# Another slot order, clamped-distance pairs by content, and score tiles partly filled by VectorE, in a fused attention and mixture-of-experts kernel

## The chip, the cores and the metric

The kernel runs on one core of a Trainium2 chip. The metric is the device time of one execution in microseconds, the median of several runs. The profile is of one further execution, with the time of each instruction on the five engines: PE (TensorE, the matrix engine; PEld is its loading of stationary operands), DVE (VectorE), ACT (ScalarE), POOL (GpSimd) and SP (SyncE, which here issues nearly all transfers).

## The reference

Sixteen sequences of 512 tokens with 256 features go through an adaptive LayerNorm, self-attention with 16 heads of 16, a second LayerNorm, and a mixture of eight experts of which each token uses two. All is float32. What matters here are the attention scores with relative positions:

```python
scores = jnp.einsum('bhqd,bhkd->bhqk', q, k)
dist_idx = pos_l - pos_r + M - 1            # M = 256, S = 512
pos_emb = dist_emb[dist_idx]
rel_q = jnp.einsum('bhld,lrd->bhlr', q, pos_emb)
rel_k = jnp.einsum('bhrd,lrd->bhlr', k, pos_emb)
scores = (scores + rel_q + rel_k) / jnp.sqrt(jnp.asarray(D, scores.dtype))
probs = jax.nn.softmax(scores, axis=-1)
```

The table dist_emb has 511 rows, and an index out of range takes the nearest row. All pairs whose query is 255 or more positions after the key thus use row 510. Call it e. For these pairs the three terms are q·k + q·e + k·e, which equals (q + e)·(k + e) − e·e.

## The kernel before, in words

**The prologue** (until about 490 us) normalizes the inputs, projects them to q, k and v, stores these in DRAM, rearranges q and k for the position terms (`stationary`), and works the first ten *pair blocks* off.

**Pair blocks** make the position terms rel_q + rel_k. A block (`Rel`, number n of 64) is 64 queries by 128 keys for the 128 pairs of batch and head of one half s of the batches; `at(n)` gives half, query block lb, key block rb and half lh of the query block. `q_set` (matmul L165, "pq" in the profile) makes rel_q for 16 queries in four PSUM banks, one for each group t of 32 rows of the array, and four ScalarE copies (L175) move them to an SBUF block `two[n % 2]` ("r"). `k_set` (L186, "pk") makes rel_k in four banks in the same way, and four VectorE additions (L195) add them to r. `store` (L203) writes 16 queries of r to rel_d in DRAM in 1 MB. Four of each make a block. A store has runs of 128 floats in DRAM.

**Units** are 128 queries of one sequence; there are 64, and each takes 16 *slots*. In groups g of four heads: `load_scores` (L582) reads position terms for 4 x 512 scores a query into a tile s, in one transfer. `content` makes q·k in four banks (L644, "qk"), and VectorE adds s to each, scales, and keeps the maximum of each row (L650); the negated maximum is the bias of `exps` (L660, ScalarE). `turn` transposes the four probability tiles on PE (L669, "pt") and ScalarE copies each out (L671). `context` multiplies them with v (L684, "pc") in a bank of its own.

The unit before goes through its second part in the same slots. `back`, `contextT` and `project` finish the attention (pcl, pct, ph). `project` copies ph on ScalarE (L738), and takes its statistics on VectorE (L741) and the inverse root on POOL (L101). `residual` scales on VectorE (L750) and makes three POOL operations (L751 to L753). `norm2` follows with statistics, an inverse root on POOL and xn (L765). `modulate`, `route`, `mask_t` and `bias` prepare the experts. `experts` multiplies for two experts at once into one bank (L827, "fpy"), and `expert_sums` adds the first half on VectorE (L838, "fy") and scales the second on ScalarE (L842, "ye"); POOL adds up ye. `mask_q` (L614, POOL) makes the two masked copies of q for the next unit.

**The order** is written by hand. `at(slot, order, fn, ...)` puts a call in a slot, and the calls of a slot are issued by their order number. The engines then take their instructions in that order. Slots repeat by fours, once for each head group. Modulo 4, PE's order was:

- slot 0: pt, then qk of the next group
- slot 1: pt, then pc of the last group
- slot 2: pt, pq, fpy (and exps of two head tiles on ScalarE, after the pq copies)
- slot 3: fy and ye, then pk, then pt (and two more exps)

Work that comes once per unit (ph in slot 7, fpt in 11, fpl in 13 and so on) lies between. Block n = u + 10 is made during unit u.

All PSUM tiles but pc's come from one pool of seven banks, `bank()`, taken in turn: a matmul group that takes a bank waits until the readers of the bank taken seven allocations earlier are done. A transfer on SP uses one of eight completion lanes in turn, and waits for the last on its lane.

## Time and profile before

| | |
|---|---|
| median of 3 runs | 2924.61 us (2921.96 to 2926.6) |
| profiled execution, its time / its span | 2935.72 / 2934.0 us |
| busy: PE, PEld | 2770.9 us (94%), 1803.2 us (61%) |
| busy: DVE, ACT, POOL | 1837.4 us (63%), 2068.8 us (71%), 630.1 us (21%) |
| granted TensorE clock, mean | 0.971 |
| SP's queue: moved, share of 16 engines | 790.03 MB, 85.2% |
| position terms: stores, loads | 256 of 1 MB each |

The busy share of a waiting matmul group needs care: its first matmuls can have begun while the others wait, and the record shows the group as busy. The shares are means over a prologue, a middle in which every unit carries a pair block, and a tail of ten units without one.

### The profile page before, as it was taken

Reading aid. Unit: us, or ns where it says so; the run is one execution under the profiler, and the core shown is the slowest. Engines: PE = TensorE matmul, PEld = TensorE weight load, DVE = VectorE, ACT = ScalarE, POOL = GpSimd, SP = SyncE. Lnnn points to the kernel's source line nnn. Section 1 sums busy time; section 2 is a strip of 40 time slices with the busy share of each in tenths; the row PEclk is TensorE's granted clock in tenths of the full one; section 3 lists DMA queues with packets and bytes.
Section 4 is the critical chain, followed back from the end, with each engine's and each line's share of the span. In section 5 each row is a group of like instructions: output and inputs, shape, how many; then the busy total and the mean of one; then the engine's idle time right before and its main releaser. Section 6 shows DMA issues by size and latency. Waiting matters only on the chain.

```text
span 2934.0 us, 76492 instructions
## 1 busy us (share of the span) xinstructions
PE 2770.9 (94%) x30186; PEld 1803.2 (61%) x30186; DVE 1837.4 (63%) x5140; ACT 2068.8 (71%) x3938; POOL 630.1 (21%) x863
## 2 busy tenths in 40 slices
PE   8779963999999999999999999999999999999997
PEld 5556642666666666666666666666666666665654
DVE  5446542666666666666666666666666666675553
ACT  2345432877777777777777777777777777777774
POOL 1000000022222222222222222222222222223333
PEclk9989876999999999999999999999999999999998
DMA  6879998688988998899888998889899898897561
GB/s 181 306 253 317 296 299 273 223 276 283 286 282 277 294 307 279 274 285 292 281 278 286 291 289 281 278 285 288 278 286 307 279 286 281 278 278 264 201 238 43
DMA packets 855350, 796.49 MB, mean 271 GB/s; under 512 B 25545, under 2 KB 649409, under 8 KB 854737
## 3 DMA queue, kind: packets, MB, share of 16 engines
q1 hardware_dynamic: 854032, 790.03, 85.2%
q8 instruction: 240, 3.93, 0.5%
q10 hardware_dynamic: 960, 1.57, 0.2%
q14 instruction: 118, 0.96, 0.1%
HBM read 462.20 MB, written 328.25 MB: 269 GB/s over the span
## 4 chain that ended last, share of the span: by engine, by line
PE 77%; DMA 2%; POOL 2%; DVE 1%; SPq 1%; ACT 1%; issue 1%; POOLq 0%; DVEq 0%; ACTq 0%
PE pt L669 18%; PE fpy L827 15%; PE qk L644 12%; PE pq L165 10%; PE pc L684 8%; PE pk L186 8%; PE ph L732 2%; DMA vu<-v_d 1%; PE fpl L788 1%; PE pcl L699 1%; PE fpb L818 1%; PE fpt L775 1%; POOL qm L614 1%; PE pct L716 0%; POOL rstd L101 0%
## 5 line engine op out<-in xcount | busy, mean ns | idle before, releaser
L671 ACT COPY pT<-pt 128x512 f32<-128x512 f32 x1024 | 595.3, 584 | 317.9 <-PE pt L669 295.3
L195 DVE TENSOR_TENSOR r<-pk,r 128x512 f32<-128x512 f32 x1024 | 635.0, 683 | 189.2 <-PE pk L186 164.3
L660 ACT ACTIVATE s<-s,mx 128x512 f32<-128x512 f32 x1024 | 689.7, 731 | 43.3 <-DVE mx L654 39.7
L650 DVE CUSTOM_DVE_ANT_0 s<-qk,s 128x512 f32<-128x512 f32 x1024 | 644.1, 685 | 85.8 <-PE qk L644 81.4
L669 PE MATMUL pt<-ident,s 128*128 128x128 f32 x4096 | 660.0, 284 | 10.8 <-ACT s L660 10.4
L175 ACT COPY r<-pq 128x512 f32<-128x512 f32 x1024 | 525.6, 603 | 153.9 <-PE pq L165 137.1
L669 PEld LDWEIGHTS pt<-ident,s 128*128 128x128 f32 x4096 | 450.0, 143 | 284.7 <-ACT s L660 73.8
L827 PE MATMUL fpy<-we_sb,fhT 128*128 128x512 f32 x1024 | 506.1, 617 | 0.0
L848 POOL TENSOR_TENSOR ye<-ye,ye 128x256 f32<-128x256 f32 x192 | 140.5, 732 | 1597.4 <-ACT ye L842 1105.8
L838 DVE SCALAR_TENSOR_TENSOR fy<-fpy,fmask,fy 128x256 f32<-128x256 f32 x256 | 123.5, 482 | 471.6 <-PE fpy L827 319.3
L644 PE MATMUL qk<-k,qm 32*128 32x512 f32 x2048 | 380.1, 650 | 28.0 <-POOL qm L614 28.0
L186 PEld LDWEIGHTS pk<-t_f,ke 32*128 32x128 f32 x8192 | 268.3, 190 | 189.5 <-ACT r L175 124.1
L165 PE MATMUL pq<-t_r,qe 32*128 32x256 f32 x4096 | 370.5, 409 | 4.2 <-DMA qe<-eq_d 2.8
L186 PE MATMUL pk<-t_f,ke 32*128 32x128 f32 x8192 | 319.8, 287 | 8.8 <-DVE r L195 3.6
L827 PEld LDWEIGHTS fpy<-we_sb,fhT 128*128 128x128 f32 x1024 | 175.0, 190 | 195.2 <-issue 159.8
L165 PEld LDWEIGHTS pq<-t_r,qe 32*128 32x128 f32 x4096 | 240.2, 186 | 82.4 <-issue 41.7
L684 PE MATMUL pc<-pT,vu 128*32 128x128 f32 x8192 | 279.1, 277 | 0.0
L684 PEld LDWEIGHTS pc<-pT,vu 128*32 128x32 f32 x8192 | 209.9, 110 | 44.1 <-issue 43.5
L644 PEld LDWEIGHTS qk<-k,qm 32*128 32x128 f32 x2048 | 133.4, 184 | 101.5 <-DVE r L195 47.6
L101 POOL TENSOR_TENSOR rstd<-rstd,mhalf 128x1 f32<-128x1 f32 (+1 forms) x144 | 87.9, 610 | 436.0 <-DVE rstd L100 428.1
L842 ACT ACTIVATE ye<-fpy,fmask 128x256 f32<-128x256 f32 x256 | 125.3, 490 | 51.3 <-DVE fy L838 51.3
L614 POOL TENSOR_SCALAR qm<-qs,par 128x256 f32<-128x256 f32 x128 | 117.7, 932 | 150.1 <-DMA k<-k_d 137.8
(110 smaller groups left out, 2061.7 us busy)
## 6 DMA issues: line engine op xcount, KB each, us to landing
rel_d<-r SPq DMA_DIRECT2D x256, 1024.0 KB, 8.5
s<-rel_d SPq DMA_DIRECT2D x256, 1024.0 KB, 7.8
vu<-v_d SPq DMA_DIRECT2D x64, 576.0 KB, 7.5
ke<-ek_d SPq DMA_DIRECT2D x128, 256.0 KB, 7.2
k<-k_d SPq DMA_DIRECT2D x128, 256.0 KB, 6.6
gt<-gates_d SPq DMA_DIRECT2D x64, 256.0 KB, 4.7
v_d<-v SPq DMA_DIRECT2D x16, 576.0 KB, 6.4
xt<-in_x SPq DMA_DIRECT2D x16, 512.0 KB, 5.9
```

Of the source, the lines that this page charges most:

```text
L165: nc.tensor.matmul(bs[t][:, a * 256 : (a + 1) * 256], e[32 * t : 32 * t + 32, (g % 2) * 2 + a, :], t_r[32 * t : 32 * t + 32, :, m0 : m0 + RK],
L175: nc.scalar.copy(dst[:, t], bs[t].rearrange("p (a c) -> p a c", a=2))
L186: nc.tensor.matmul(bs[t][:, a * 128 : (a + 1) * 128], e[32 * t : 32 * t + 32, a, :], t_f[32 * t : 32 * t + 32, :, m0 : m0 + LQ], start=Tru ...
L195: nc.vector.tensor_tensor(dst, bs[t].rearrange("p (r l) -> p l r", r=8), dst, ALU.add)
L614: nc.gpsimd.tensor_scalar(qm[:, pa], qs, par[:, pa : pa + 1], None, ALU.mult)
L644: nc.tensor.matmul(bs[t], t_["q"][rows, pa, cc, :], t_["k", cc][rows, :], start=True, stop=True)
L650: nc.vector.tensor_tensor_reduce(st[:, t, :], bs[t], st[:, t, :], 0.25, -3.0e38, ALU.add, ALU.max, mx[:, t : t + 1],)
L660: nc.scalar.activation(t_["s", g][:, t, :], t_["s", g][:, t, :], AF.Exp, bias=t_["m", g][:, t : t + 1])
L669: nc.tensor.transpose(pt[:, cols], t_["s", g][:, t, cols], ident)
L671: nc.scalar.copy(pT, pt)
L684: nc.tensor.matmul(pc[32 * t : 32 * t + 32, g, :], t_["v"][:, rb, h * VW : h * VW + 32], pTs[t][:, rb * P : (rb + 1) * P], start=(rb == 0) ...
L827: nc.tensor.matmul(py, t_["hT"][:, kc, :], we_sb[:, kc, pr * 2 * E : (pr + 1) * 2 * E], start=(kc == 0), stop=(kc == NE - 1),)
```

## The change

1. *Pairs at the clamped distance.* For query block 3 and key block 0 all distances are 257 or more. The four blocks with n % 32 in 24, 25 are left out (`todo`, 60 blocks). For query block 3, `content` uses two matmuls for each t: the plain one for the last 384 keys, and one with q + e (`qf`, made on POOL) and k + e (`shift_k`, in place, on POOL) for the first 128. The −e·e is put in the score tile by VectorE.
2. *rel_d's layout.* It is now [head, key block, query, 128 keys]. A store of 16 queries is one run of 8 KB a head, and the load of a head group is four transfers, one for each head, with runs of 512 B.
3. *Another order of the four slots*, and pq's four copies in two pairs. Modulo 4 it is now: slot 0: pt, pc, qk; slot 1: pt; slot 2: pt, fpy, the first exps, fy and ye, pq and its first two copies; slot 3: pt, pq's other two copies, pk, the other three exps.
4. *One buffer* instead of two for the first ye of a unit (`ye0`).

The core of it:

```diff
-    rel_d = [dram.tile([P, P, S], F32, tag=f"rel_{n}", name=f"rel_d{n}") for n in range(8)]
+    rel_d = [dram.tile([P, NL, P, RK], F32, tag=f"rel_{n}", name=f"rel_d{n}") for n in range(8)]
...
+            self.todo = [n for n in range(64) if n % 32 // 2 != 12]
...
+            self.banks = bs
+            self.q_copy(n, g, (0, 1))
+
+        def q_copy(self, n, g, ts):
...
-            for t in range(4):
-                nc.scalar.copy(dst[:, t], bs[t].rearrange("p (a c) -> p a c", a=2))
+            for t in ts:
+                nc.scalar.copy(dst[:, t], self.banks[t].rearrange("p (a c) -> p a c", a=2))
...
-                out=rel_d[s * 4 + lb][:, l0 : l0 + 16, rb * RK : (rb + 1) * RK],
+                out=rel_d[s * 4 + lb][:, rb, l0 : l0 + 16, :],
...
-        nc.sync.dma_start(
-            out=st, in_=rel_d[s * 4 + lb][h0 : h0 + 7 : 2].rearrange("h l r -> l h r")
-        )
+        rb0 = lb // 3
+        r0 = RK * rb0
+        for t in range(4):
+            nc.sync.dma_start(
+                out=st[:, t, r0:].rearrange("p (rb r) -> p rb r", r=RK),
+                in_=rel_d[s * 4 + lb][h0 + 2 * t, rb0:].rearrange("rb l r -> l rb r"),
+            )
+        if r0:
+            nc.vector.tensor_copy(
+                st[:, :, 0:r0], minus_ee.unsqueeze(2).to_broadcast([P, 4, r0])
+            )
...
+    def shift_k(u, cc):
+        kt = units[u]["k", cc]
+        nc.gpsimd.tensor_scalar(kt[:, 0:RK], kt[:, 0:RK], far, None, ALU.add)
...
+        if place(u)[1] == 3:
+            qf = u1.tile([P, 2, NE, P], F32, tag="qf", name=f"qf_{u}")
+            for pa in range(2):
+                nc.gpsimd.tensor_scalar(
+                    qf[:, pa], qs, far, par[:, pa : pa + 1], ALU.add, ALU.mult
+                )
...
+            r0 = RK if "qf" in t_ else 0
             nc.tensor.matmul(
-                bs[t], t_["q"][rows, pa, cc, :], t_["k", cc][rows, :], start=True, stop=True
-            )
+                bs[t][:, r0:], t_["q"][rows, pa, cc, :], t_["k", cc][rows, r0:],
+                start=True, stop=True,
+            )
+            if r0:
+                nc.tensor.matmul(
+                    bs[t][:, 0:r0], t_["qf"][rows, pa, cc, :], t_["k", cc][rows, 0:r0],
+                    start=True, stop=True,
+                )
...
-        ye = u2.tile([P, E], F32, tag=f"ye{pr > 0}", name=f"ye_{u}_{pr}")
+        ye = (u2 if pr else u1).tile([P, E], F32, tag=f"ye{pr > 0}", name=f"ye_{u}_{pr}")
...
             at(q0 - 4, 5, content, u, g)
-            at(q0 - 2, 7, exps, u, g, (0, 1))
-            at(q0 - 1, 7, exps, u, g, (2, 3))
+            at(q0 - 2, 6.3, exps, u, g, (0,))
+            at(q0 - 1, 5, exps, u, g, (1, 2, 3))
             for t in range(4):
                 at(q0 + t, 3, turn, u, g, t)
-            at(q0 + 5, 4, context, u, g)
+            at(q0 + 4, 4, context, u, g)
...
+        if u % 32 // 8 == 3:
+            at(z - 8, 0, shift_k, u, 0)
+            at(z - 2, 0, shift_k, u, 1)
...
-        at(z + 16, 7, bias, u)
+        at(z + 17, 6, bias, u)
         for pr in range(4):
             at(z + 18 + 4 * pr, 6, experts, u, pr)
-            at(z + 19 + 4 * pr, 1, expert_sums, u, pr)
+            at(z + 18 + 4 * pr, 6.6, expert_sums, u, pr)
...
-                at(z + 2 + 4 * g, 4, rel.q_set, n, g)
-                at(z + 15 + 4 * g, 2, rel.k_set, n, g)
+                at(z + 2 + 4 * g, 7, rel.q_set, n, g)
+                at(z + 3 + 4 * g, 3.5, rel.q_copy, n, g, (2, 3))
+                at(z + 15 + 4 * g, 4, rel.k_set, n, g)
```

The rest of the diff makes `far` (e on the 128 rows) and `minus_ee` in the prologue, where all four pq copies still follow `q_set` at once, and counts the blocks by `todo`.

More of the change, by code (lines that the diff above doesn't have):

```diff
@@ L94, in adaln_attention_moe_kernel @@
     t_r = const.tile([P, 2, 2 * S], F32, name="t_r")
+    far = const.tile([P, 1], F32, name="far")
+    minus_ee = const.tile([P, 4], F32, name="minus_ee")
     wo_sb = const.tile([P, NE, E], F32, name="wo_sb")
@@ L131, in __init__, with at @@
             self.ke = {}
+            self.todo = [n for n in range(64) if n % 32 // 2 != 12]
             self.two = [rblk.tile([P, LQ, RK], F32, name=f"r_{i}") for i in range(2)]
-        @staticmethod
-        def at(n):
-            s, m = n // 32, n % 32
+        def at(self, n):
+            s, m = self.todo[n] // 32, self.todo[n] % 32
             return s, m // 8, m % 8 // 2, m % 2
@@ L142, in wants @@
             w = []
-            if rb == 0:
+            if rb == lb // 3:
                 w += [("q", s, lb * 2 + lh, g) for g in range(2)]
@@ L383, in blocks @@
                 rel.q_set(n, g)
+                rel.q_copy(n, g, (2, 3))
                 for w in ahead:
@@ L514, in adaln_attention_moe_kernel @@
                     )
+            far_row = su.tile([P, D], F32, name="far_row")
+            last = dist_t[:, 510:511]
+            with nc.allow_non_contiguous_dma(reason="one column of the table"):
+                nc.sync.dma_start(
+                    out=far_row, in_=last.rearrange("d o -> (o d)").partition_broadcast(P)
+                )
+            for h in range(8):
+                nc.sync.dma_start(out=far[h * D : (h + 1) * D, :], in_=last)
+            nc.vector.tensor_tensor(far_row, far_row, far_row, ALU.mult)
+            nc.vector.tensor_reduce(
+                minus_ee, far_row.unsqueeze(1).to_broadcast([P, 4, D]), AX.X, ALU.add
+            )
+            nc.vector.tensor_scalar(minus_ee, minus_ee, -1.0, None, ALU.mult)
             m8 = su.tile([P, 8], F32, name="m8")
@@ L581, in load_scores @@
         st = sp.tile([P, 4, S], F32, tag="s", name=f"s_{u}_{g}")
-        nc.sync.dma_start(
-            out=st, in_=rel_d[s * 4 + lb][h0 : h0 + 7 : 2].rearrange("h l r -> l h r")
-        )
+        rb0 = lb // 3
+        r0 = RK * rb0
+        for t in range(4):
+            nc.sync.dma_start(
+                out=st[:, t, r0:].rearrange("p (rb r) -> p rb r", r=RK),
[5 more added lines that the diff above has]
+            )
         units[u]["s", g] = st
@@ L615, in mask_q @@
         units[u]["q"] = qm
+        if place(u)[1] == 3:
[4 more added lines that the diff above has]
+                )
+            units[u]["qf"] = qf
     def load_rest(u):
@@ L643, in content @@
             rows = slice(32 * t, 32 * t + 32)
+            r0 = RK if "qf" in t_ else 0
             nc.tensor.matmul(
-                bs[t], t_["q"][rows, pa, cc, :], t_["k", cc][rows, :], start=True, stop=True
-            )
+                bs[t][:, r0:], t_["q"][rows, pa, cc, :], t_["k", cc][rows, r0:],
+                start=True, stop=True,
+            )
+            if r0:
+                nc.tensor.matmul(
+                    bs[t][:, 0:r0], t_["qf"][rows, pa, cc, :], t_["k", cc][rows, 0:r0],
+                    start=True, stop=True,
+                )
         mx = u3.tile([P, 4], F32, tag="mx", name=f"mx_{u}_{g}")
@@ L899, in adaln_attention_moe_kernel @@
         n = u + LEAD
-        if n < NP:
+        if n < len(rel.todo):
             for g in range(4):
-                at(z + 2 + 4 * g, 4, rel.q_set, n, g)
-                at(z + 15 + 4 * g, 2, rel.k_set, n, g)
+                at(z + 2 + 4 * g, 7, rel.q_set, n, g)
+                at(z + 3 + 4 * g, 3.5, rel.q_copy, n, g, (2, 3))
+                at(z + 15 + 4 * g, 4, rel.k_set, n, g)
             for g in range(4):
                 at(z + 28 + 2 * g, 0, rel.store, n, g)
-        if n + 1 < NP:
+        if n + 1 < len(rel.todo):
             for w in rel.wants(n + 1):
```

## The prediction

> **What bounds the kernel now.** I read the page's engine rows first, then its chain of work that ended last, then one stretch in the middle and one near the end.

> ```profile
> span 2934.0 us, 76492 instructions
> PE 2770.9 (94%) x30186; PEld 1803.2 (61%) x30186; DVE 1837.4 (63%) x5140; ACT 2068.8 (71%) x3938; POOL 630.1 (21%) x863
> PE 77%; DMA 2%; POOL 2%; DVE 1%; SPq 1%; ACT 1%; issue 1%; POOLq 0%; DVEq 0%; ACTq 0%
> 1400.00:1600.00 200.00, 199.99 (x2337) 129.55 (x2341) 133.41 (x370) 157.28 (x302) 47.42 (x65) 1.00 0.90 281
> 2700.00:2800.00 100.00, 94.04 (x923) 60.42 (x923) 57.82 (x198) 76.95 (x148) 33.33 (x46) 0.98 0.65 230
> ```

> TensorE sets the time: 199.99 of 200 us busy in mid-kernel. But a group of matmuls that waits for one PSUM bank still counts as busy, so I took the timeline of one unit (repeats every 39.1 us) and measured from each group's start to the next one's. Around the LayerNorms it reads, PE first, then DVE, POOL and ACT:

> ```profile
> 1520.97 1.17 PE L186 MATMUL pk<-t_f,ke 32*128 32x128 f32 x32
> 1527.47 2.02 PE L165 MATMUL pq<-t_r,qe 32*128 32x256 f32 x16
> 1529.42 1.98 PE L827 MATMUL fpy<-we_sb,fhT 128*128 128x512 f32 x4
> 1531.33 1.17 PE L186 MATMUL pk<-t_f,ke 32*128 32x128 f32 x32
> ...
> 1522.16 2.49 DVE L195 TENSOR_TENSOR r<-pk,r 128x512 f32<-128x512 f32 x4 [0.60 <-PE pk L186]
> 1524.57 0.42 DVE L741 BATCH_NORM_STATS2 stats<-ph 128x6 f32<-128x256 f32 x1
> 1531.28 0.42 DVE L765 TENSOR_SCALAR xn<-x,mv,rstd 128x256 f32<-128x256 f32 x1 [1.18 <-POOL rstd L101]
> 1531.61 0.48 DVE L838 SCALAR_TENSOR_TENSOR fy<-fpy,fmask,fy 128x256 f32<-128x256 f32 x1
> ...
> 1526.56 0.74 POOL L751 TENSOR_TENSOR x<-x,gt 128x256 f32<-128x256 f32 x1 [0.53 <-DVE x L750]
> 1528.88 1.83 POOL L614 TENSOR_SCALAR qm<-qs,par 128x256 f32<-128x256 f32 x2
> 1530.68 0.57 POOL L101 TENSOR_TENSOR rstd<-rstd,mhalf 128x1 f32<-128x1 f32 x1
> ...
> 1529.11 2.06 ACT L175 COPY r<-pq 128x512 f32<-128x512 f32 x4 [0.89 <-PE pq L165]
> 1532.26 0.49 ACT L842 ACTIVATE ye<-fpy,fmask 128x256 f32<-128x256 f32 x1
> ```

> The same pq group takes 1.08 us start to start where nothing holds it; here 1.95. Over the four groups of the unit, qk and pq lose 2.4 us above 1.08 (qk 0.54 and 0.75; pq 0.08, 0.18 and 0.87). The cause is the ring of seven PSUM banks: the last bank of qk is the one that pk's third VectorE add (L195) empties, seven allocations earlier; pq's last bank is emptied by the third score reduction. So mid-kernel is about 36.7 us of matmuls plus 2.4 us of such waits. The second thing to see is a long chain: stats (24.57), POOL's gate products, POOL's qm, POOL's rstd (30.68), xn, fy (ends 32.09). It is 7.52 us, and today it delays nobody in mid-kernel. In the tail, with less PE work, it does:

> ```profile
> 2858.50 0.44 PE L775 MATMUL fpt<-ident,xn 128*128 128x128 f32 x2 [1.86 <-DVE xn L765]
> ```

> [...] in the trace ye never begins less than 0.035 us after fy's end, in 256 pairs. [...] So everything behind a waiting ye on ScalarE waits too. [...] the gaps of 1.86 us in the tail go with a granted clock of 0.98. I add nothing for that.

> **The change part by part.** T is a transpose group, F the expert matmul (fpy); t is microseconds from where pk could start.

> *Slot order.* PE ran T, qk, T, pc, T, pq, F, pk, T. It becomes T, pc, qk, T, T, F, pq, T, pk. Switch costs: T takes 0.49 before T or F and 0.58 before others; 0.1 per group less, 0.4 per unit. qk's last banks now come from pk's first two adds, with T (0.58) and pc (1.01) between: no wait. pq's banks come from score reductions with T, T, F (2.9 us) between: none. Those 2.4 us go. But pk's third and fourth banks are now the two that pq's first copies empty, with only one T between. From the rows: the first copy starts 1.16 us after pq does, the second 0.48 later (four take 2.06), and takes 0.60: free at 2.24, with semaphore 2.28. PE reaches pk at 1.08 + 0.58 = 1.66. Wait 0.62, in every group. The four a-rounds of pk issue in order, so the whole pk slips, and the adds begin at t = 1.57 instead of 1.19.

> *fy and ye move before pq's copies.* In an ordinary group this is hidden: fy starts 0.11 after F's successor, ends 0.59, ye runs 0.63 to about 1.1, the first copy is due at 1.16. In the LayerNorm group it isn't. ScalarE, in order, does two pq copies, T's copy, two pq copies, three exps (0.62 apart), then the copy of ph: it ends at t = 4.16, and the bn_stats on the same bank follows at 4.2. Plus 7.52: fy ends at 11.72. PE meanwhile: pk to 1.72, ph 1.11, T 0.58, pc 1.01, qk 1.08, T and T 0.98, F 1.91, pq 1.08, T 0.58: ready for pk at 10.05. ye starts 11.76, copies at 12.16 and 12.64, the second ends 13.24: pk's last bank opens at 13.28, a wait of 3.2. In the router group nine small VectorE instructions (1.38 us) stand between the reductions and fy: fy ends about 1.1 us after F, the wait is 1.0. Sum per unit: 0.62 + 0.62 + 3.2 + 1.0 = 5.5, for 2.4 + 0.4 gained: period 41.8, **+2.7 us**. About 49 periods have pair work: **+132**.

> *Four pair blocks left out.* Four periods with pair work become periods without. The last ten units of before run at 28.5 or 30.1, mean 29.3: 4 x (39.1 - 29.3) = **-39**. Their adds, copies, stores and stationary loads go with them.

> *Content with q+e and k+e.* 256 matmuls become 512 of 384 and 128 columns: the columns are the same, and pk shows that 128-column matmuls on four row groups cost no extra (32 in 1.10 us). Nothing added, at most 0.2 us x 64 = 13. On POOL, qf is two more instructions like qm (0.93 each) and the shift of k is half of one (0.5): 2.4 us ahead of rstd in the chain above, so fy and pk are later by that much in 16 units: **+38**. The second shift lies in a stretch where POOL idles. The VectorE fill (512 elements, like a 0.68 us row) comes 64 times, ahead of the score reductions; VectorE is 63% busy and pq has 0.4 us to spare: nothing, at most 40.

> *rel_d's layout and four loads for one.* A 1 MB store goes from 2048 packets of 512 B to 128 of 8 KB. In the trace's packet records 512 B take 28.7 ns, 2 KB 96, 8 KB 309 (medians and means near each other): over 16 engines 3.7 us becomes 2.5. A load goes from 512 packets of 2 KB (3.1 us) to 2048 of 512 B (3.7). Per unit that is -4.8 and +2.4: 35 us of DMA work become 32.5, in a longer period. In mid-kernel transfers are early, so nothing. In the prologue, from 220 to 490 us, the DMA share is 0.9 to 1.1 and 40 stores lie there, worth 48 us; I take **-35** (bounds 0 and -55). SP issues 12 more DMAs a unit at about 0.45 us: 5.4 us; the waits of its stores alone (565.9 us in 58) show 10 us of slack a unit. The small setup loads: 0 to 3.

> *Tail.* Without pq and pk, pc comes one slot earlier and needs T's copy, which is behind ye: reductions and negation end 2.8 us after qk, exp0, then fy and ye end at 4.0, T's copy at 4.5, while PE is there at 4.1: 0.4 to 0.5 a group. In the LayerNorm group ph's copy is behind three exps, so the 1.86 us gap grows by about 1. Some 32.2 us a unit for 29.3, 14 units: **+41**.

> *ye with one buffer.* Its last reader ends some 2.5 us into the four slots before the next writer: nothing; if not, up to 1 us a unit.

> **Sum.** 2934 - 35 + 132 - 39 + 38 + 41 = 3071 for the profiled execution. The execution profiled took 2935.7 against a median of 2924.6, so the median is 9 less than this sum: **3062**.

> **The rivals.** (1) *Faster: fy does not hold the copies.* Place: fy, ye, pq's copies. It decides if the 7.5 us chain finishes before F ends, at t = 8.4, that is, if it were 4.2 us shorter. Then each wait is 0.62: 4 x 0.62 - 2.4 - 0.4 = -0.3 a unit, -15; with -35, -39 and +10 in the tail, about 2846. For it: the chain costs nothing in mid-kernel now. Against: xn waits 1.18 us for POOL there, and fy is behind xn in the built order. (2) *DMA becomes the bound.* 33 DMAs a unit on eight completion lanes, each waiting for the one eight before it. At the 7.8 us to landing of today 33 x 7.8 / 8 = 32 us, plus 10 of waits: 42, just the new period. If 512 B reads land in 10 us it is 51 a unit, about 3500. Against: fewer bytes are queued ahead of each. (3) *Half of it*: the three exps and the copy of ph overlap better than I have it, or the shifts find POOL idle: about 2990.

> **How the numbers follow.** The forecast's mechanism 0.70, half of it 0.11, DMA 0.04, the faster one 0.12, balance near zero 0.03. Between runs this kernel varies by 0.16%, so 0.2% is what can be told from no change. Slower 0.85, same 0.03, faster 0.12. The forecast's own range is 3010 to 3125 (prologue 0 to -55, fill and content 0 to +50, tail 0 to +60). The half case takes it down to 2940, and I stop there, as what lies below and above is under 2 in 10; upper end 3130.

> **What would show it.** qk and pq groups at 1.08 us or a little more; pk groups at 1.7 us in two of four, about 2.1 after the router and 4.3 after the LayerNorm; PE's waits named ACT r or ACT ye at pk; DMA share down to about 0.8; the first pair of qk some 35 us earlier; period 41.8. Wrong would be: pk at 1.10 after the LayerNorm (then rival 1), s loads as the releaser of the score reductions (rival 2), a period below 39.1.

## The result, and the profile after

The changed kernel takes **3219.47 us** (median of 4 runs, 3218.88 to 3224.17) against 2925.61 us of the kernel before in the same session (4 runs, 2921.96 to 2928.58). The ratio is 1.1009, with a 95% interval of 1.099 to 1.1028: ten per cent slower. The forecast had the direction, and the place of the new waits, but its rise of 137 us is less than half of the 294 us measured.

The profiled execution spans 3217.2 us, 283.2 more than before. First the page of the changed kernel: the engine rows, the shares of engines in the chain of work that ended last, and SP's queue.

```profile
span 3217.2 us, 77690 instructions
PE 2927.8 (91%) x29930; PEld 1935.5 (60%) x29930; DVE 1823.6 (57%) x5143; ACT 2021.2 (63%) x3874; POOL 665.3 (21%) x927
q1 hardware_dynamic: 734112, 754.43, 73.0%
PE 12%; POOL 4%; DVE 3%; issue 2%; DMA 2%; ACT 1%; SPq 1%; POOLq 0%; DVEq 0%; ACTq 0%
```

ScalarE and VectorE do less than before in a longer span, and SP's queue falls from 85.2% to 73.0% of the engines' time. So no engine and no queue has become fuller. The chain explains only a quarter of the span by name (before, PE alone was 77% of it), so it doesn't say where the time went. The view by stretches (length, busy time of PE, PEld, DVE, ACT and POOL, granted TensorE clock, DMA share, GB/s) shows a stretch in the middle and one in the tail:

```profile
1000.00:1200.00 200.00, 192.50 (x2092) 125.03 (x2090) 122.16 (x336) 138.70 (x269) 43.56 (x60) 0.97 0.82 262
2900.00:3000.00 100.00, 82.19 (x821) 57.66 (x820) 49.08 (x166) 61.78 (x118) 32.54 (x47) 0.90 0.51 154
```

Before, PE was busy for 199.99 of 200 us in mid-kernel, with 2337 matmuls at a clock of 1.00. Now it begins 2092, has 7.5 us with nothing at all, and its clock is 0.97.

The unit shows why. This is the timeline of the group around the LayerNorms, the stretch that the forecast was made from (start, duration, engine, line, operation; in brackets the idle time before it and what ended it):

```profile
1100.27 1.78 PE L194 MATMUL pk<-t_f,ke 32*128 32x128 f32 x32
1106.69 1.88 PE L877 MATMUL fpy<-we_sb,fhT 128*128 128x512 f32 x4
1108.50 1.47 PE L169 MATMUL pq<-t_r,qe 32*128 32x256 f32 x16
1110.49 0.48 PE L194 MATMUL pk<-t_f,ke 32*128 32x128 f32 x2
1112.51 2.95 PE L194 MATMUL pk<-t_f,ke 32*128 32x128 f32 x30 [1.54 <-ACT ye L892]
1115.39 0.69 PE L825 MATMUL fpt<-ident,xn 128*128 128x128 f32 x2
...
1104.43 0.43 DVE L791 BATCH_NORM_STATS2 stats<-ph 128x6 f32<-128x256 f32 x1
1111.14 0.41 DVE L815 TENSOR_SCALAR xn<-x,mv,rstd 128x256 f32<-128x256 f32 x1 [1.17 <-POOL rstd L104]
1111.47 0.48 DVE L888 SCALAR_TENSOR_TENSOR fy<-fpy,fmask,fy 128x256 f32<-128x256 f32 x1
...
1111.98 0.47 ACT L892 ACTIVATE ye<-fpy,fmask 128x256 f32<-128x256 f32 x1 [1.99 <-DVE fy L888]
1112.35 1.06 ACT L183 COPY r<-pq 128x512 f32<-128x512 f32 x2
```

From bn_stats (1104.43) to the end of fy (1111.95) it is again 7.52 us, as before. But fpy, which fy reads, ended at 1108.5, so fy comes 2.9 us late, ye follows fy, the first two copies of pq follow ye, and pk stands between 1110.97 and 1112.51 with its first two matmuls issued. The single records of pk show which banks it waits for: its second bank is that of fpy and opens with the end of ye (1112.45, pk goes on at 1112.51), and its third and fourth are those of pq's first two copies (these end at 1112.93 and 1113.41, pk goes on at 1112.98 and 1113.47). The list of PE's waits (total us, times, longest) has one such wait in each of the 48 middle units, and the one of fpt is the tail's:

```profile
PE pk L194 <- ACT ye L892: 85.3, 48, 3.0
PE fpt L825 <- DVE xn L815: 63.6, 14, 5.4
```

Those records give only the part in which PE did nothing. From each group's start to the next one's, worked out from the timeline for unit 12 and others in mid-kernel, the four groups of a unit take, in us:

| | before | after, unit 11 | after, unit 12 | forecast |
|---|---|---|---|---|
| qk | 0.96 / 1.62 / 1.07 / 1.84 | 1.72 / 1.07 / 1.07 / 2.15 | 1.73 / 1.07 / 1.07 / 1.07 | 1.08 each |
| pq | 1.16 / 1.26 / 1.95 / 1.08 | 1.08 / 1.08 / 1.40 / 1.08 | 1.08 / 1.08 / 1.40 / 1.08 | 1.08 each |
| pk (last two: LayerNorm, router) | 1.10 / 1.10 / 1.10 / 1.11 | 1.71 / 1.71 / 4.06 / 1.71 | 1.71 / 1.71 / 4.90 / 2.36 | 1.7 / 1.7 / 4.3 / 2.1 |
| whole unit | 39.1 | 42.8 | 43.9 | 41.8 |

Units 11 and 12 do the same work. They differ in the clock. Of the 40 middle units without query block 3, 6 take 42.8 and the other 34 take 43.9 to 45.1. Short windows over unit 12 (same columns as above) show what the longer ones have:

```profile
1110.00:1112.00 2.00, 0.97 (x6) 0.61 (x6) 0.81 (x2) 0.02 (x1) 1.10 (x2) 1.00 0.49 179
1112.00:1114.00 2.00, 1.49 (x14) 1.12 (x18) 0.00 (x0) 2.00 (x5) 0.72 (x1) 0.90 0.02 7
1114.00:1116.00 2.00, 2.00 (x26) 1.77 (x22) 0.92 (x2) 2.00 (x5) 0.00 (x0) 0.50 0.00 0
1116.00:1118.00 2.00, 2.00 (x41) 1.47 (x39) 1.57 (x3) 1.89 (x5) 0.00 (x0) 0.75 0.00 0
```

Just after the stall TensorE runs at half clock, for some 3.4 us (0.4, 2.0 and 1.0 us of the last three rows). Over the middle units these windows sum to 194.6 us (before: 0), over the tail to 100.0 us (before: 29.7). All 34 of the longer ordinary units have one or two, and the 6 shorter ones none.

### The profile page after: what moved, and what is told of

The parts are those of the page before. It is cut to its first block, busy times and chain, and to the rows that moved or that the text cites. A ratio compares the mean times of both kernels' runs of the same rounds, so it can differ in the third digit from the quotient of the medians.

```text
span 3217.2 us, 77690 instructions
## 1 busy us (share of the span) xinstructions
PE 2927.8 (91%) x29930; PEld 1935.5 (60%) x29930; DVE 1823.6 (57%) x5143; ACT 2021.2 (63%) x3874; POOL 665.3 (21%) x927
## 3 DMA queue, kind: packets, MB, share of 16 engines
q10 hardware_dynamic: 960, 1.57, 0.1%
## 5 line engine op out<-in xcount | busy, mean ns | idle before, releaser
L203 DVE TENSOR_TENSOR r<-pk,r 128x512 f32<-128x512 f32 x960 | 594.9, 682 | 612.3 <-PE pk L194 454.0
L719 PEld LDWEIGHTS pt<-ident,s 128*128 128x128 f32 x4096 | 474.4, 146 | 282.4 <-issue 155.2
L194 PE MATMUL pk<-t_f,ke 32*128 32x128 f32 x7680 | 506.3, 308 | 91.2 <-ACT ye L892 85.3
L194 PEld LDWEIGHTS pk<-t_f,ke 32*128 32x128 f32 x7680 | 394.6, 200 | 205.3 <-ACT ye L892 95.0
L688 PE MATMUL qk<-k,qm 32*128 32x512 f32 (+1 forms) x2048 | 336.1, 648 | 22.6 <-DMA s<-rel_d 22.6
L734 PE MATMUL pc<-pT,vu 128*32 128x128 f32 x8192 | 329.9, 302 | 6.4 <-ACT pT L721 5.9
L169 PE MATMUL pq<-t_r,qe 32*128 32x256 f32 x3840 | 317.2, 405 | 4.1 <-DMA qe<-eq_d 3.1
L169 PEld LDWEIGHTS pq<-t_r,qe 32*128 32x128 f32 x3840 | 203.1, 185 | 184.0 <-issue 43.7
L734 PEld LDWEIGHTS pc<-pT,vu 128*32 128x32 f32 x8192 | 239.7, 120 | 71.4 <-issue 47.3
L688 PEld LDWEIGHTS qk<-k,qm 32*128 32x128 f32 x2048 | 104.4, 199 | 102.0 <-issue 56.6
```

The source lines that it names most:

```text
L169: nc.tensor.matmul(bs[t][:, a * 256 : (a + 1) * 256], e[32 * t : 32 * t + 32, (g % 2) * 2 + a, :], t_r[32 * t : 32 * t + 32, :, m0 : m0 + RK],
L194: nc.tensor.matmul(bs[t][:, a * 128 : (a + 1) * 128], e[32 * t : 32 * t + 32, a, :], t_f[32 * t : 32 * t + 32, :, m0 : m0 + LQ], start=Tru ...
L203: nc.vector.tensor_tensor(dst, bs[t].rearrange("p (r l) -> p l r", r=8), dst, ALU.add)
L688: nc.tensor.matmul(bs[t][:, r0:], t_["q"][rows, pa, cc, :], t_["k", cc][rows, r0:], start=True, stop=True,)
L719: nc.tensor.transpose(pt[:, cols], t_["s", g][:, t, cols], ident)
L734: nc.tensor.matmul(pc[32 * t : 32 * t + 32, g, :], t_["v"][:, rb, h * VW : h * VW + 32], pTs[t][:, rb * P : (rb + 1) * P], start=(rb == 0) ...
```

## The experiments

Twelve kernels. Where a ratio is given it is to the kernel before, on the same chip, with a 95% interval. "Middle" is the time over 48 unit periods that carry pair blocks (1877.7 us before, 2130.8 after), "tail" what follows (491.7 and 529.0).

**1. The order alone.** The kernel before, with nothing but the new slot order and pq's copies in two pairs; no block is left out, the layout is the old one.

```diff
-            for t in range(4):
+            for t in ts:
...
-            at(q0 - 2, 7, exps, u, g, (0, 1))
-            at(q0 - 1, 7, exps, u, g, (2, 3))
+            at(q0 - 2, 6.3, exps, u, g, (0,))
+            at(q0 - 1, 5, exps, u, g, (1, 2, 3))
...
-            at(q0 + 5, 4, context, u, g)
+            at(q0 + 4, 4, context, u, g)
...
-            at(z + 16, 7, bias, u)
+            at(z + 17, 6, bias, u)
...
-            at(z + 19 + 4 * pr, 1, expert_sums, u, pr)
+            at(z + 18 + 4 * pr, 6.6, expert_sums, u, pr)
...
-                at(z + 2 + 4 * g, 4, rel.q_set, n, g)
-                at(z + 15 + 4 * g, 2, rel.k_set, n, g)
+                at(z + 2 + 4 * g, 7, rel.q_set, n, g)
+                at(z + 3 + 4 * g, 3.5, rel.q_copy, n, g, (2, 3))
+                at(z + 15 + 4 * g, 4, rel.k_set, n, g)
```

> The kernel before with only the new order of the four slots. If the order alone costs what the changed kernel's ordinary units show (43.6 us on the average for 39.1): 53 periods of +4.5, eleven tail units of +4, together 3200 to 3220, with the clock in mid-kernel at 0.96 to 0.97 and pk at 1.7, 1.7, 4.9 and 2.4 us. If it needs the other parts to do harm (the four loads, the fill): below 3100.

Measured: 3228.34 us, ratio 1.1024 (1.099 to 1.1058). The middle takes 2107.6 us, 43.9 a unit, and the LayerNorm's pk group takes 4.08 us in the units at full clock. The stretch in mid-kernel has about the clock and the PE time of the changed kernel (0.97 and 192.50):

```profile
1000.00:1200.00 200.00, 193.63 (x2090) 126.99 (x2091) 119.34 (x324) 140.00 (x272) 40.97 (x57) 0.95 0.84 263
```

The unit is as expected; the time is 8 us above the range expected, and the clock 0.01 below it. The order by itself costs 300 us, which is as much as the whole change.

**2. Everything but the order.** The changed kernel with the old slot numbers put back; left-out blocks, content by q + e and k + e, the fill, the layout and the single ye buffer stay.

```diff
-            at(q0 + 4, 4, context, u, g)
+            at(q0 + 5, 4, context, u, g)
...
-            at(z + 18 + 4 * pr, 6.6, expert_sums, u, pr)
+            at(z + 19 + 4 * pr, 1, expert_sums, u, pr)
...
-                at(z + 2 + 4 * g, 7, rel.q_set, n, g)
-                at(z + 3 + 4 * g, 3.5, rel.q_copy, n, g, (2, 3))
-                at(z + 15 + 4 * g, 4, rel.k_set, n, g)
+                at(z + 2 + 4 * g, 4, rel.q_set, n, g)
+                at(z + 2 + 4 * g, 4, rel.q_copy, n, g, (2, 3))
+                at(z + 15 + 4 * g, 2, rel.k_set, n, g)
```

> The changed kernel with the slot order of before; the left-out blocks, the content with q + e and k + e, the layout of rel_d and its four loads stay. Order as the cause: four blocks less (-39), the prologue as in the changed kernel (-6), up to +20 for the longer POOL chain in 16 units: 2880 to 2915. Transfers or the content as the cause: above 3100.

Measured: 2937.15 us, ratio 1.0025 (1.0014 to 1.0036). Ordinary units take 39.1, as expected. The total is 22 us above the range expected, and the units of query block 3 are why: 41.6 in the middle and 32 to 33 in the tail, where ordinary tail units take 28.5 or 30.1. In the tail their gap ahead of fpt has become

```profile
2665.37 0.52 PE L825 MATMUL fpt<-ident,xn 128*128 128x128 f32 x2 [3.70 <-DVE xn L815]
```

where the tail of before showed 1.86. So the other parts together gain nothing: the prologue is 3 us shorter and the tail 15, the middle 20 longer, and what the left-out blocks save is spent again in sixteen units. Experiments 9 to 11 take that apart.

**3. The second LayerNorm behind the experts' sums.** The changed kernel with norm2 (bn_stats, POOL's rstd, xn) issued after fy and ye in its slot, so that fy no longer stands behind xn on VectorE.

```diff
-        at(z + 10, 0, norm2, u)
+        at(z + 10, 6.8, norm2, u)
```

> The changed kernel with norm2 issued after expert_sums in its slot, so that fy and ye no longer stand behind xn on VectorE. Waits at pk as the cause: the pk group after the second LayerNorm falls from 4.9 us to about 1.7, the granted clock in mid-kernel returns to 1.00, the period goes from 43.6 (46.8 for query block 3) to about 39.3, and the time to 2940 to 2980. Transfers as the cause (four loads for one, 512 B runs): nothing of this is touched, so above 3150. Clock gating with another origin: the clock stays near 0.95 in mid-kernel and the time above 3100.

Measured: 3066.74 us, ratio 1.0471 (1.0453 to 1.0489), 153 us less than the changed kernel; 40.7 a unit. The same group on PE:

```profile
1115.62 1.47 PE L169 MATMUL pq<-t_r,qe 32*128 32x256 f32 x16
1117.60 2.04 PE L194 MATMUL pk<-t_f,ke 32*128 32x128 f32 x32
1121.39 2.22 PE L688 MATMUL qk<-k,qm 32*128 32x512 f32 x8
```

and the stretch in mid-kernel:

```profile
1000.00:1200.00 200.00, 199.92 (x2225) 127.72 (x2223) 130.34 (x360) 148.44 (x290) 46.76 (x65) 1.00 0.87 278
```

pk falls from 4.06 and more to 1.97, and the clock is back at 1.00 (17.1 us of half clock in the whole middle, for 194.6, and none in ordinary units). So fy does hold the copies, and the low clock is a consequence of that stall and no cause of its own. The time is 87 us above the range expected. The expected 39.3 a unit was too low by 1.4, and qk explains most of it: 2.15 us after the LayerNorm, 1.73 after the router. For the first of these the list of waits in this stretch names the releaser:

```profile
PEld qk L688 <- ACT fhT L827: 0.8, 1, 0.8
```

ScalarE's fhT, which empties the bank of fpt, stands behind the three exps that the new order puts into slot 3. One bank of qk is reused from it. ScalarE ends fhT at 1122.43, and qk goes on at 1122.47. After the router the bank is that of fpmt, and its reader fmaskT (1084.30 to 1084.54 in the changed kernel) stands behind the three exps too; the rest of qk starts at 1084.59.

**4. A dose on POOL, in both kernels.** One more POOL operation of 128x256 at the end of residual; it multiplies by 1.0. In the changed kernel it lengthens the chain to fy, in the kernel before it lengthens the same chain.

```diff
         nc.gpsimd.tensor_tensor(x2, x2, t_["x"], ALU.add)
+        nc.gpsimd.tensor_scalar(x2, x2, 1.0, None, ALU.mult)
```

The changed kernel with it:

> The changed kernel with one more POOL instruction (128x256 by 1.0, about 0.9 us) in each unit between the first norm's products and the second root; its result is unchanged. If fy, ye and pq's copies hang on POOL's chain, every unit grows by the whole 0.9 us: +55 to +65, 3275 to 3290. If the wait at pk has another source: within 10 of 3219.

The kernel before with it:

> The same extra POOL instruction in the kernel before. There fy has 0.4 us to spare before pk's adds, and xn more: the period grows by about 0.5 (39.1 to 39.6), the ten units of the tail by 0.9: +30 to +40, about 2960. If the order of before hides the chain wholly: 2925 to 2935.

Measured: 3299.52 us in the changed kernel (ratio 1.1263, 1.1241 to 1.1286), 80 more than without; 2973.33 in the kernel before (ratio 1.0156, 1.0136 to 1.0175). The stall in the changed kernel:

```profile
1130.25 0.48 PE L194 MATMUL pk<-t_f,ke 32*128 32x128 f32 x2
1133.22 2.93 PE L194 MATMUL pk<-t_f,ke 32*128 32x128 f32 x30 [2.49 <-ACT ye L893]
```

The added operation takes 0.86 us. It lengthens the chain from bn_stats to the end of fy from 7.52 to 8.46 us in both kernels. In the changed kernel the recorded idle time grows from 1.54 to 2.49 and the group from 4.90 to 5.83, by 0.95 and 0.93. So there POOL's chain sets the wait of PE one for one. The whole loses 80 us for the 55 to 65 expected; half-clock windows now sum to 266 us in the middle, for 194.6. In the kernel before a middle unit takes 39.5 for 39.1: all but 0.4 was covered there. Of its loss, 43 us for the 30 to 40 expected, 19.5 are in the middle and 20.2 in the tail.

**5. ye behind the copies.** The changed kernel with ye split off from fy and issued after pq's first two copies on ScalarE.

```diff
+    def expert_sums2(u, pr):
+        t_ = units[u]
+        py = t_.pop("py")
+        e = 2 * pr
...
             at(z + 18 + 4 * pr, 6.6, expert_sums, u, pr)
+            at(z + 18 + 4 * pr, 7.5, expert_sums2, u, pr)
```

> The changed kernel with ye issued behind pq's first two copies on ScalarE; fy stays. If the copies wait because they are behind ye: the pk group after the second LayerNorm opens when fpy's bank is read by ye, 1 us earlier or more (4.9 to about 3.1, and fewer windows of half clock), while the ordinary pk groups, which then wait for the later ye, go from 1.7 to about 2.05; together 3080 to 3150. If ye's place is of no account: 3219.

Measured: 3184.48 us, ratio 1.087 (1.0848 to 1.0892). The groups came out as expected: pk 2.09 / 2.08 / 3.11 / 2.08 (now ye and T's copy stand ahead of pq's last copies), and pk's recorded idle time is

```profile
1107.29 1.00 PE L194 MATMUL pk<-t_f,ke 32*128 32x128 f32 x6
1109.32 1.15 PE L194 MATMUL pk<-t_f,ke 32*128 32x128 f32 x26 [1.02 <-ACT ye L897]
```

But the unit takes 42.9, and 43.4 where a half-clock window follows: in the units at full clock qk is at 2.14 after the LayerNorm, the wait for fhT that unit 12 of the changed kernel doesn't show, since its PE comes there later. The total gained 35 us, less than the 70 to 140 expected. Shortening the wait at pk uncovered the one at qk.

**6. The experts' matmuls behind pq.** The changed kernel with fpy, fy and ye after pq, its copies and T, just ahead of pk.

```diff
-            at(z + 18 + 4 * pr, 6, experts, u, pr)
-            at(z + 18 + 4 * pr, 6.6, expert_sums, u, pr)
+            at(z + 19 + 4 * pr, 3.6, experts, u, pr)
+            at(z + 19 + 4 * pr, 3.7, expert_sums, u, pr)
```

> The changed kernel with fpy, fy and ye moved to the next slot, between pt and pk. Waits of pk for pq's copies as the cause: fpy's 1.9 us now cover the copies, fy and ye stand behind nothing that waits long, so pk is at 1.1 us in all four groups, period 36 to 37, time 2750 to 2800, under both kernels. If another limit lies close beneath (ScalarE, 71% busy before, or the transfers), the period stays above 38 and the time above 2850.

Measured: 3031.79 us, ratio 1.0346 (1.0329 to 1.0364); 40.9 a unit. pk is at 1.10 in all four groups, as expected. But the whole was expected below the kernel before, at 2750 to 2800, and this failed:

```profile
1105.52 1.14 PE L688 MATMUL qk<-k,qm 32*128 32x512 f32 x8
1107.83 2.56 PE L169 MATMUL pq<-t_r,qe 32*128 32x256 f32 x16
1112.63 1.17 PE L194 MATMUL pk<-t_f,ke 32*128 32x128 f32 x32
```

pq now comes 2.3 us after qk, and its banks are the ones that the score reductions empty, which end at 1109.2. pq goes on then, and takes 2.49 to the next group. fpy had covered that time. The period and the time are those of the other branch of the expectation, but the limit met is neither ScalarE nor the transfers. Over the unit pq takes 8.1 (1.61 / 2.49 / 2.53 / 1.48) for 4.6 in the changed kernel. The waits of the ring of banks changed places when the work moved: pk's are gone (1.10), and pq's came where fpy had stood.

**7. The layout alone.** The kernel before with rel_d as [head, key block, query, 128 keys], and four loads for one.

```diff
-    rel_d = [dram.tile([P, P, S], F32, tag=f"rel_{n}", name=f"rel_d{n}") for n in range(8)]
+    rel_d = [dram.tile([P, NL, P, RK], F32, tag=f"rel_{n}", name=f"rel_d{n}") for n in range(8)]
...
-        nc.sync.dma_start(
-            out=st, in_=rel_d[s * 4 + lb][h0 : h0 + 7 : 2].rearrange("h l r -> l h r")
-        )
+        for t in range(4):
+            nc.sync.dma_start(
+                out=st[:, t, :].rearrange("p (rb r) -> p rb r", r=RK),
+                in_=rel_d[s * 4 + lb][h0 + 2 * t].rearrange("rb l r -> l rb r"),
+            )
```

> The kernel before with only rel_d's new layout and four loads for one. If the transfers play no part in mid-kernel the period stays 39.1, the first qk comes 15 to 25 us earlier, and the time is about 2905. If they cost: a period of 40 or more, time above 2950. If the 35 us that were forecast for the prologue come in full without the set-up of e, 2890.

Measured: 2916.76 us, ratio 0.9958 (0.9941 to 0.9975), a gain of 0.4%. A middle unit stays at 39.1: half as many transfers again on SP's queue (2289 for 1521) are hidden, as the forecast had it. The gain is the prologue's, 13 us for the 15 to 25 expected: the first qk comes at 478.1 for 491.2. The stretch in question, 220 to 490 us, is, before and then here

```profile
220.00:490.00 270.00, 196.15 (x2018) 136.76 (x2016) 132.81 (x293) 107.19 (x201) 4.17 (x5) 0.82 0.98 296
220.00:490.00 270.00, 204.95 (x2068) 140.95 (x2065) 138.51 (x313) 111.92 (x210) 6.00 (x7) 0.82 0.85 309
```

The DMA share falls from 0.98 to 0.85 while the rate rises from 296 to 309 GB/s: the stores do cost less time on the DMA engines, but PE gets ahead by 13 us only.

**8. The set-up of e later.** The changed kernel with the loads and the three small VectorE operations for e moved behind the preparation of the third input in the prologue.

```diff
-            far_row = su.tile([P, D], F32, name="far_row")
-            last = dist_t[:, 510:511]
...
+            far_row = su.tile([P, D], F32, name="far_row")
+            last = dist_t[:, 510:511]
```

> The changed kernel with the set-up of e (nine small transfers and three VectorE instructions) after the third sequence's preparation instead of ahead of it. It delays the early prologue by 14 us in the changed kernel. If that delay lasts: first qk 10 to 14 us earlier, 3205 to 3210. If it is taken up by the transfers that bound the prologue later: within 4 us of 3219.

In the changed kernel VectorE stands for a transfer of 16 floats to each partition, and the inputs' LayerNorms stand behind it:

```profile
61.38 0.17 DVE L532 TENSOR_TENSOR far_row<-far_row 128x16 f32<-128x16 f32 x1 [17.28 <-DMA far_row<-in_dist_t]
```

PE's fifth group of transposes of the prologue starts at 80.81 for 66.70, 14.1 us late. Measured with the set-up moved: 3219.51 us, ratio 1.0982 (1.0955 to 1.1009), the same as without, which is the second of the two cases expected; the fifth group is still 5.7 us late and the sixth 8.4, and the first qk comes at 485.3 for 485.2. So the delay is real at 80 us and no longer decides at 485. Why the ten kernels with the set-up of e (484.0 to 493.1) do not reach the 478.1 of the layout alone stays open. Part of it may be chance: experiment 1 and the second kernel of experiment 4 have the prologue of before, and their first qk comes at 487.6 and 486.7 for 491.2.

**9. The shifted q and the first shifted k behind the second root.** The changed kernel with qf and the first shift of k issued on POOL after norm2 instead of ahead of it, in the units of query block 3.

```diff
-            at(z - 8, 0, shift_k, u, 0)
+            at(z - 5, 0, shift_k, u, 0)
+            at(z - 5, 0, far_q, u)
```

> The changed kernel with q + e (qf) and the first shift of k made on POOL after the second root instead of ahead of it, so that in the 16 units of query block 3 the chain to xn is as short as in the others. The POOL chain as the cause of their longer period: 46.8 falls to about 43.9 in mid-kernel and the tail's units by 1 to 2 us, in all -30 to -40, 3180 to 3190. If it is the split matmuls or the VectorE fill: no change, 3219.

This stretch of the changed kernel shows POOL in the unit at 1640 us:

```profile
1640.83 0.60 POOL L629 TENSOR_SCALAR k<-k,far 128x128 f32<-128x128 f32 x1
1641.41 1.82 POOL L649 TENSOR_SCALAR qm<-qs,par 128x256 f32<-128x256 f32 x2
1643.23 1.08 POOL L655 TENSOR_SCALAR qf<-qs,far,par 128x256 f32<-128x256 f32 x2
1644.28 0.56 POOL L104 TENSOR_TENSOR rstd<-rstd,mhalf 128x1 f32<-128x1 f32 x1
```

Measured with them behind rstd: 3178.22 us, ratio 1.0849 (1.0828 to 1.0871), 41 us less than the changed kernel. Middle units of query block 3 take mostly 44.0 to 44.1 for a mean of 46.6; ordinary units stay at 43.9. That is a little more than the 30 to 40 expected, and with the POOL work out of the way neither the split matmuls nor the fill show in these units. So 1.7 us of POOL work in the chain, sixteen times, cost 2.6 us each.

**10. The old order, with the fill late.** Experiment 2 with the VectorE fill of the score tile issued behind the reductions of its slot.

```diff
+            if u % 32 // 8 == 3:
+                at(q0 - 12, 5.5, fill, u, g)
```

> The changed kernel with the slot order of before, and the fill of the score tiles on VectorE moved behind the score reductions of its slot. In that kernel without the move the units of query block 3 took 41.6 us in mid-kernel where others took 39.1, with pq at 1.6 to 2.3 us. If the 0.41 us fill ahead of the reductions is the cause: 39.1 to 39.5 for these, in all about -18, 2919. If it is POOL's chain: no change, 2937.

Measured: 2928.46 us, ratio 0.9993 (0.9984 to 1.0001). Middle units of query block 3 fall from 41.6 to 40.5, less than half of the way to the 39.1 to 39.5 expected; the tail doesn't move. The fill is 0.41 us, four times a unit, and costs 1.1 a unit where it stands ahead of the reductions.

**11. The old order, with fill, qf and first shift late.** Experiment 10 with the edit of experiment 9: the left-out blocks, the layout and content by q + e and k + e in the order of before, with each of the added operations where nobody waits for it.

> The changed kernel with the slot order of before, the fill behind the score reductions, and q + e and the first shift of k behind the second root. Without the fill's move these units took 41.6 us in mid-kernel and 32 to 33 in the tail, with it 40.5 and 32 to 33. If what is left is POOL's chain: 39.1 to 39.4 in mid-kernel, 28.5 to 31 in the tail, time 2880 to 2900, below both kernels. If it is the split matmuls: 2920 to 2930.

Measured: **2899.42 us**, ratio **0.9895** (0.9879 to 0.9912): faster than both kernels, by 1.0% and by 10%. The middle is 1878.7 us (39.1 a unit, query block 3 too), the tail 454.4 for 491.7. The stretch with the units of query block 3, in the changed kernel and then here, is full again:

```profile
1500.00:1780.00 280.00, 262.05 (x2938) 183.81 (x2936) 165.84 (x467) 183.10 (x355) 71.67 (x103) 0.93 0.67 218
1500.00:1780.00 280.00, 279.98 (x3464) 193.48 (x3456) 194.88 (x547) 219.78 (x422) 78.52 (x111) 1.00 0.83 267
```

## Why the prediction was right and wrong

**Right: that it is slower, and by which mechanism.** fy behind xn behind POOL, ye behind fy (in 256 pairs of the changed kernel ye never begins less than 0.034 us after fy's end), pq's copies behind ye (above, ScalarE is idle for 1.99 us until fy ends, runs ye at 1111.98, and begins the first copy at 1112.35), pk behind the copies. Experiment 1 gives the loss to the order alone, experiment 3 cuts the chain at one place and takes out 153 us, experiment 4 lengthens it by one POOL operation and finds just this in pk. The forecast put the wait on pk's third and fourth banks, which is right for its end; that pk's second bank is fpy's, so that ye holds pk directly too, it did not see. Ordinary groups of pk were forecast at 1.7 and take 1.71; the LayerNorm's at 4.3, 4.06 to 4.08 where the clock is full; the router's at 2.1, 1.71 at full clock and 2.36 else.

**The rivals.** The faster one, that fy does not hold the copies, is refuted by the same runs. (By the forecast's own numbers, an end of the chain at 11.72 and of F at 8.4, the chain would have to be 3.3 us shorter for this, not 4.2.) DMA as the bound is refuted by experiment 7, in which the same four loads for one leave a unit at 39.1, and by the order alone, which loses as much with the old loads. Of the half case neither ground held: the LayerNorm's wait had the length forecast, and POOL was not idle under the shifts.

**Wrong: the size.** The span grew by 283.2 us, the forecast sum by 137. The miss of 146 has three places: the prologue (-7.2 to the first unit's fpmt, for -35) 27.8; the middle (+253.1, for 132 x 48/49 + half of 38 = 148.3) 104.8; and the tail (+37.3, for 41 - 39 + the other half of 38 + one period's 2.7 = 23.7) 13.6.

*The middle.* Three steps failed: the clock, put at nothing, and two waits in the ring of banks, put at nothing.
- "I add nothing for that" was said of gaps and clock. It was the author's estimate, made beside gaps of 1.86 us in the tail and a mean clock of 0.98 there. The measurement decides: a recorded idle time of 1.54 us with two matmuls issued ahead of it came with a half-clock window in 34 of 40 units. The kernel before had it already: of eight tail units with a gap of 1.86 to 2.27 us ahead of fpt, four have a half-clock window, and these are the units of 30.1 us or more, the other four being those of 28.5. The gap at 2858.50 that the forecast shows is one of them:

```profile
2860.00:2864.00 4.00, 4.00 (x47) 2.49 (x41) 2.70 (x9) 2.72 (x6) 0.15 (x1) 0.57 0.70 244
```

The mean of 0.98 over 100 us hid this; a window there costs 30.1 - 28.5 = 1.6 us. The price in the middle is 43.9 - 42.8 = 1.1 us a unit, after what qk no longer waits in the slowed units.
- "qk's last banks now come from pk's first two adds ... no wait" counted the banks strictly in turn and left out fpt and fpmt, which take a bank between pk and qk. The waits in the trace show that the banks do not come strictly in turn: qk's last bank after the LayerNorm goes on with the end of fhT, and its third after the router with the end of fmaskT, though fpt and fpmt are fewer than seven allocations earlier. What sets this order the runs do not show. These ScalarE readers stand behind three exps: 0.65 us in the group after the router in each unit, and 1.08 after the LayerNorm in those that come there at full clock. Experiment 3 shows both waits without the stall.
- "pq's banks come from score reductions with T, T, F between: none" holds in three groups. In the LayerNorm's the reductions begin behind the first LayerNorm's statistics and root and end at 1108.8, where pq was ready at 1108.5: 0.32.

At full clock these make 0.65 + 1.08 + 0.32 = 2.05 more than forecast, pk makes 0.24 + 0.39 less, and some 0.4 less is fpy, at 1.81 for 1.91 in each of four groups: 42.8 for 41.8. So at full clock the unit is 1.0 above the forecast, and the half-clock windows add 1.1 to most units: of the middle's miss the ring and the clock have about equal parts. (Of the forecast's +132, three us are rounding: its four waits add to 5.44, not 5.5.) For query block 3 the 2.4 us of added chain was near the truth by luck: qf takes 0.54 for each half and not 0.93, the shift 0.60, so the chain has 1.7 of work more and is 1.8 longer (9.30 for 7.52); the units take 46.64 - 43.94 = 2.7 more, and most of them have a second window of low clock. Experiment 9, which takes the 1.7 away, gains 41 us; 38 were forecast.

*The prologue.* "I take -35" took three quarters of the DMA time saved as time of PE. The 48 us saved were themselves too many: 28.7 and 96 ns are means and 309 is a median; with the mean of 8 KB packets, 337 ns in the trace before, it is 39. The layout alone brings the first qk 13 us nearer. "The small setup loads: 0 to 3" were 14 at 80 us of the prologue, though not at its end. Between 13 and the 6 of the changed kernel the cause is not settled.

*The tail.* 32.2 us a unit were forecast; 33.7 to 34.2 and, with query block 3, 35.1 to 36.1 were measured. The wait of PE for xn ahead of fpt, forecast to grow from 1.86 by about 1, sums to 63.6 us there (22.4 before), with 100 us of low clock (29.7 before). How the miss divides between that wait and the clock the runs do not show.

*The fill and the content.* "Nothing, at most 40" for the fill was not measured apart in the changed order, but in experiment 9, which keeps it and the split matmuls, the middle units of query block 3 have a mean of 44.1 us for 43.8 of the others, so there it is near nothing. In the old order, where pq waits for just those reductions, it is 1.1 us in each of the eight middle units, 8.5 in the middle in all. The split matmuls and the single ye buffer cost nothing that shows: with both, experiment 11 has 39.1 us a unit.

*The four blocks left out.* -39 stands: with the added work out of the way (experiment 11) the middle is as before (1878.7 for 1877.7), and the tail, to which the four periods belong, is 37.3 us shorter.

## What to carry to other kernels

In a ring of PSUM banks shared by all groups, ask for each group which reader empties the bank it gets (the waits in the trace tell, a count in turn may not), what stands ahead of this reader in the program of its engine, and how much PE work lies between; in experiments 3, 5 and 6 taking out one wait uncovered the next (2.15 us at qk, 2.14 at qk, 2.49 at pq), so re-count the whole ring, the small once-a-unit groups included. One POOL operation more in the side chain, 0.94 us longer for it, cost 0.4 us a unit in the old order, and 0.93 at pk in the new one, where PE's feedback path is queued behind the chain's end: put its consumer after the instructions that free banks. And look in the profile of the kernel as it is for what PE stalls of a microsecond or two already do to the clock, stall by stall, before a new one is priced at nothing.

## What the runs showed of the hardware

| | idle time at pk, us | units with a half-clock window |
|---|---|---|
| second LayerNorm behind the sums (experiment 3) | none above 0.5 | 0 of 40 |
| ye behind the copies (5) | 1.02 | 24 of 40 |
| changed kernel | 1.54 | 34 of 40 |
| changed kernel, one POOL operation more (4) | 2.49 | 40 of 40 |

The length alone does not decide: ahead of fpt in the tail, gaps of 1.86 to 2.27 us bring a window in 4 of 8 units of the kernel before, and gaps of 1.83 to 1.86 us in 1 of 8 of the layout alone (7).

- In the changed kernel, up to the units of query block 3, the window begins about 0.5 us later in each following unit, counted from the unit's start (31.3, 31.8, 32.3, 32.8 us after fpmt), until a unit has none and it begins at 31.5 again. In following units the windows begin 44.37 us apart, 0.47 more than the 43.9 of the unit, and this is the drift. What sets this distance was not shown.
- On POOL the operation with two scalar operands was the quicker one: qf, (q + e) times a mask on 128x256, takes 0.541 to 0.552 us in 32 instances; qm with one scalar from a tile takes 0.92 on the same shape, and the product with a constant of experiment 4 takes 0.86.
- Where one bank of a group isn't free, the matmuls ahead of it in the program begin and those behind it wait as well, and part of the wait is recorded as busy: pk's four banks open at 1110.49, 1112.51, 1112.98 and 1113.47, and its recorded idle time is 1.54 us in a group that takes 3 us more than the 1.10 it takes where nothing holds it.
